# Loading the next block's x in quarters, and one more block with seven products

## The chip, the cores and the metric

The kernel runs on one core of one Trainium2 chip. The metric is device time in microseconds (us), from the start of the program to its end. The kernel before takes 1078.87 us, the median of 3 runs that lie between 1078.11 and 1079.22.

In what follows PE is the matrix engine, DVE, ACT and POOL are the vector, scalar and general engines, and SP is the engine whose only work here is to issue loads from memory. Each engine works through its own instructions in program order and waits on semaphores that the others count up.

## The reference

For 128 samples, x has 64 channels by 512 positions. Each sample picks one of 200 matrices, 64 by 64, and is mixed over its channels with it. A two-layer network follows over the 512 positions, whose weights are first rounded to three values (-1, 0, +1, times one factor alpha per matrix). The result is quantized to 4 bits with one scale for the whole tensor, and x is added:

```
w = weights[conditions];  z = einsum('bct,bcd->bdt', x, w)
h = gelu(einsum('bsd,hd->bsh', z, ternarize(W1)) + b1)      # 512 -> 2048
y = einsum('bsd,hd->bsh', h, ternarize(W2)) + b2            # 2048 -> 512
scale = max(|y|) / 7 + 1e-8
out = x + clip(round(y / scale), -7, 7) * scale
```

The scale needs every y before any output can be written.

## The kernel before, in words

**Tiling.** Two samples make a pair (128 rows), four pairs make a block of 512 token columns, and there are NB = 16 blocks, 0 to 15. The hidden width of 2048 is cut into NH = 16 chunks of 128. The ternary weights stay in on-chip memory in 8 bits and are widened by POOL, chunk by chunk, just before PE uses them (`widen1`, `widen2`, `widen7`). Every activation is held as a high and a low part, so each product is done twice, once with each.

**Memory.** The pool `big` (line 92) has 20 buffers of 8 KB per partition, and `half` (line 94) has 10 of half that size. Each finished block leaves its y in one big buffer until the end. So the later the block, the fewer big buffers are free.

**Layer 1 in two forms.** `eight` (line 881) does one hidden chunk at a time in the plain way: 8 matmuls of 512 columns for layer 1 and 8 for layer 2 (LAG = 2 chunks behind). `pair` with `seven` (lines 938 and 815) does two hidden chunks at a time and takes layer 1 as a product of 2 by 2 matrices of quarters, with seven products in place of eight (Winograd's form of Strassen's method): 28 matmuls of 256 columns for layer 1, and the same 16 of 512 columns for layer 2. I call one such call a step; a block has 8 of them, k = 0 to 7. `SEVEN` (line 88) says which blocks are done so: 2 to 11 here. A seven-block needs three big buffers for its inputs (`parts7`: `xb` and two `xt`, the sums `t` in high and low part) and one half buffer (`xl`); an eight-block needs two big ones (`parts`). The combined weights of the seven products, `w1s`, are one more big buffer.

**The next block's input.** While block n is computed, block n + 1 is prepared. SP loads its x, four pairs at once, into one big buffer (`load_x`, two transfers of 512 KB). POOL gathers the four pairs' matrices (`fetch`) and places them (`place`). Then, one pair in each of four steps, PE mixes the pair's x with its matrix into a PSUM tile `pc` (`mix`: four matmuls of the program, which the profile shows as eight records), and ACT and DVE take the parts from it: `condition` (line 232) for an eight-block, `condition7` (line 783) for a seven-block. `condition7` first copies one quarter of `pc`, `b12`, and forms four sums of quarters, `t`. They lie in a half buffer named `mixed` that all pairs share (lines 923 to 925). It then returns a last piece of work, which splits `t` into its high and low part. Inside a seven-block that piece is kept in `parting` and done one step later.

**Order.** Nothing is scheduled by a tool: the class `InOrder` (line 49) keeps every engine's instructions in the order of the source. In `pair`, the function `behind(i)` (line 953) puts the side work at six places of a step. For the change these matter: at i = 0 of step 0 the load of the next x and its buffers; at i = 2 the kept split of the pair before; at i = 4 of steps 3 to 6 the conditioning of pairs 0 to 3. In `eight` the load stands at chunk 0 and the conditioning at chunks 8 to 11, there with the split done at once.

**The end.** After block 15 the scale is found, and then all 16 blocks are quantized, added to x, which is loaded once more, and written.

Of the kernel before, what the change touches and what calls it, by code (L numbers as in the profile page):

```python
# [28 lines left out]
F32 = mybir.dt.float32  # L29
# [10 lines left out]
P = 128  # L40
# [17 lines left out]
def tile_cond_ternary_ffn(  # L58
# [26 lines left out]
    GH = NH // NG  # L85
    WCH = GH * T
    LAG = 2
    SEVEN = range(2, 12)
    HALF = BLK // 2

    const = ctx.enter_context(tc.tile_pool(name="const", bufs=1))
# [13 lines left out]
    def load_x(n):  # L105

        xt = big.tile([P, PAIRS, T], F32, tag="big", name=f"xt_{n}")
        for h in range(2):
            js = pair_of_pairs(h)
            sp.dma_start(out=xt[:, js, :], in_=x_blk[n][:, js, :])  # L110
        return [xt[:, pair_of_pairs(h), :] for h in range(2)]
# [7 lines left out]
    def split_x(n):  # L119

        return [half_x(n, h) for h in range(2)]
# [94 lines left out]
    def split(src, hi, lo, engine=dve):  # L216

        act.copy(hi, src)
        engine.tensor_tensor(lo, src, hi, ALU.subtract)

    def mix(xt, j, pc):

        for c in range(NT):
            pe.matmul(
                out=pc[:, c, :],
                lhsT=xt[j // 2][:, j % 2, c * P : (c + 1) * P],
                rhs=diag[:, j, :],
                start=True,
                stop=True,
            )  # L230

    def condition(n, j, xt, two):
        pc = ps_c.tile([P, NT, P], F32, tag="pc", name=f"pc_{n}_{j}")
        mix(xt, j, pc)
        split(pc, *(t[:, :, j * P : (j + 1) * P] for t in two))


# [115 lines left out]

    def mix0(j):
        pc = ps_y.tile([P, NT, P], F32, tag=f"py{j}", name=f"pc_0_{j}")
        mix(x_next, j, pc)
        pcs.append(pc)

    def hi0(j):
# [357 lines left out]
    for hc in range(NH - LAG):  # L717
        if hc + 2 < NH - LAG:
            widen2(0, hc + 2)
        layer2(0, hc)  # L720
        g, i = divmod(hc, GH)
        if g + 1 < NG and i in (1, 2):
            turn2(g + 1, i - 1, signs2[g + 1][:, 1, :])(act)
        if g + 2 < NG:
            if i == 0:
                made[g + 2] = signed2(g + 2)
            if i in (0, 2):
                next(made[g + 2])
        if hc in (1, 3, 5, 7):
            condition(1, hc // 2, x_next, two_next)  # L730
        if 8 <= hc < 8 + NG:
            sum2(hc - 8)
    cond[1] = two_next
# [46 lines left out]
            half.tile([P, 2, 2, HALF], F32R, tag="half", name=f"xl_{n}"),  # L780
        )

    def condition7(n, j, xt, two):

        xb, xts, xl = two
        cols = slice(j * C, (j + 1) * C)
        pc = ps_c.tile([P, NT, P], F32, tag="pc", name=f"pc_{n}_{j}")
        mix(xt, j, pc)
        t, b12 = extra["t"], extra["b12"]
        act.copy(b12, pc[:, :2, C:])  # L790
        act.copy(xb[:, 0, :, cols], pc[:, :, :C])
        act.copy(xl[:, 0, :, cols], pc[:, 2:, C:])
        dve.tensor_tensor(t[:, 0], b12, pc[:, :2, :C], ALU.subtract)
        dve.tensor_tensor(t[:, 2], pc[:, 2:, C:], b12, ALU.subtract)
        dve.tensor_tensor(t[:, 1], pc[:, 2:, C:], t[:, 0], ALU.subtract)
        dve.tensor_tensor(t[:, 3], pc[:, 2:, :C], t[:, 1], ALU.subtract)
        dve.tensor_tensor(xb[:, 1, :, cols], pc[:, :, :C], xb[:, 0, :, cols], ALU.subtract)
        dve.tensor_tensor(xl[:, 1, :, cols], pc[:, 2:, C:], xl[:, 0, :, cols], ALU.subtract)
        t8 = t.rearrange("p a c d -> p (a c) d")
        hi, lo = (x.rearrange("p a c d -> p (a c) d")[:, :, cols] for x in xts)  # L800
        return lambda: split(t8, hi, lo)

    def product(out, w, b, first):
        for c in range(2):
# [76 lines left out]
    def eight(s):  # L881

        n, hc = steps[s]
        if s + 1 < len(steps):
            ahead = steps[s + 1]
            if ahead[0] not in SEVEN:
                widen1(*ahead)
                lend(0, *ahead)
            else:
                for g in (2, 3, 0):  # L890
                    widen7(0, g)
        widen2(*steps[s + 1 - LAG])
        lend(1, *steps[s + 1 - LAG])
        if n + 1 < NB:
            if hc == 0:
                x_next.append(load_x(n + 1) if n + 1 < NB - 1 else split_x(n + 1))
                two_next.append(parts7(n + 1) if n + 1 in SEVEN else parts(n + 1))
            if 2 <= hc < 2 + PAIRS:
                fetched.append(fetch(n + 1, hc - 2))
            if 7 <= hc < 7 + PAIRS:  # L900
                place(hc - 7, fetched[hc - 7 - PAIRS])
        if n == NB - 1 and hc == 0:
            again.append(load_x(0))
        if n == NB - 1 and hc in (1, 2):
            again.append(split_x(hc))
        ph = ps_h.tile([P, BLK], F32, tag="ph", name=f"ph_{n}_{hc}")
        layer1(n, hc, ph)
        two = half.tile([P, 2, BLK], F32R, tag="half", name=f"h_{n}_{hc}")
        bend(n, hc, ph, [two[:, k, :] for k in range(2)], hf[hc % 2])
        if s + 1 < len(steps) and steps[s + 1][0] in SEVEN and n not in SEVEN:  # L910
            widen7(0, 1)
        if n + 1 < NB and 8 <= hc < 8 + PAIRS:
            if n + 1 in SEVEN:
                condition7(n + 1, hc - 8, x_next[-1], two_next[-1])()
            else:
                condition(n + 1, hc - 8, x_next[-1], two_next[-1])
            cond[n + 1] = two_next[-1]
        if hc == LAG:
            for j in range(PAIRS):
                largest(n - 1, j)  # L920
        if n + 1 == SEVEN[0]:
            if hc == 2:
                mixed = half.tile([P, 2, BLK], F32, tag="half", name="mixed")
                extra["t"] = mixed[:, 0].rearrange("p (a c d) -> p a c d", a=4, c=2)
                extra["b12"] = mixed[:, 1, : 2 * C].rearrange("p (c d) -> p c d", c=2)
                extra["making"] = combine()
            if hc in (3, 4, 5, 6):
                next(extra["making"])
        if s == len(steps) - 1:
            return  # L930
        if s == NH + 1:
            alpha_2()
        layer2(*steps[s - LAG])
        if steps[s - LAG][1] == NH - 1:
            for j in range(PAIRS):
                result(n - 1, j)

    def pair(n, k, finish):

        s = n * NH + 2 * k  # L940
        ahead = (k + 1) % (NH // 2)
        leaves = ahead == 0 and n + 1 not in SEVEN
        before = steps[s - 2], steps[s - 1]

        def second(i):
            layer2(*before[i // PAIRS], [i % PAIRS])

        def results(js):
            if before[1][1] == NH - 1:
                for j in js:  # L950
                    result(n - 1, j)

        def behind(i):
            if i == 0:
                finish()
                widen2(*before[1])
                if k == 0:
                    x_next.append(load_x(n + 1))
                    two_next.append(parts7(n + 1) if n + 1 in SEVEN else parts(n + 1))
            if i == 1:  # L960
                low(*before[1])
                if leaves:
                    widen1(n + 1, 0)
                else:
                    widen7(ahead, 1)
                    widen7(ahead, 0)
                if k < PAIRS:
                    fetched.append(fetch(n + 1, k))
                if 2 <= k < 2 + PAIRS:
                    place(k - 2, fetched[PAIRS * (n - 1) + k - 2])  # L970
            if i == 2:
                if parting:
                    parting.pop()()
                widen2(*steps[s])
                if not leaves:
                    widen7(ahead, 2)
            if i == 3:
                results(range(2))
            if i == 4:
                if not leaves:  # L980
                    widen7(ahead, 3)
                if 3 <= k < 3 + PAIRS:
                    if n + 1 in SEVEN:
                        parting.append(condition7(n + 1, k - 3, x_next[-1], two_next[-1]))
                    else:
                        condition(n + 1, k - 3, x_next[-1], two_next[-1])
                    cond[n + 1] = two_next[-1]
                if k in (1, 2):
                    for j in (2 * k - 2, 2 * k - 1):
                        largest(n - 1, j)  # L990
            if i == 5:
                results(range(2, PAIRS))

        return seven(n, k, behind, second)

    s = NH
# [110 lines left out]
```

## Time and profile before

| What | Value |
|---|---|
| profiled execution, its own time | 1079.13 us |
| its span, first to last instruction | 1077.4 us |
| median of 3 runs | 1078.87 us |
| PE busy | 999.9 us, 93% of the span |
| DVE, ACT, POOL busy | 594.8, 598.6, 613.8 us (55 to 57%) |
| PE clock granted, mean over the span | 0.969 |
| last matmuls of block 15 end | about 1010 us |
| quantizing, second load of x, output | about 1013 to 1077 us |

The profile is one execution. Its time is 1.7 us longer than its span, which is what lies around the first and last instruction. Busy time is a union over an engine's instructions. A matmul's record covers its start to its modelled end, and ends overlap the next start, so the pace of PE is read from starts. "Idle before" is time in which the engine did nothing, with the engine that ended it. Transfers are shown with the time from issue to landing. All lines of the kernel go through one helper (line 54), so instructions are told apart by the names of their tiles: `xy` and `z` are the accumulators of the seven products, `ph` that of an eight-block's layer 1, `py` those of layer 2, `pc` that of the mix, `mixed` the buffer with the sums.

### The profile page before, as it was taken

To read this page: it belongs to the slowest core of one execution; us is meant where nothing else is said; L and a number is where in the kernel's file an instruction comes from. 1 tells how busy PE (TensorE), PEld (TensorE's weight loads), DVE (VectorE), ACT (ScalarE), POOL (GpSimd) and SP (SyncE) were. 2 spreads that over 40 slices of the span, in tenths; PEclk is the share of its full clock that TensorE was granted. 3 is DMA by queue.
4 is the path that set the end of the run, shared out by engine and by line. 5 is a ranking of instruction groups with operands and counts; after the bars stand their busy time and mean duration, and the time that the engine had idled before them with its cause. 6 is when DMAs were issued, how large, how long until landed. Compare 5 with 4: busy or idle time off the path is not lost.

```text
span 1077.4 us, 16522 instructions
## 1 busy us (share of the span) xinstructions
PE 999.9 (93%) x5778; PEld 867.2 (80%) x5780; DVE 594.8 (55%) x1035; ACT 598.6 (56%) x1010; POOL 613.8 (57%) x996
## 2 busy tenths in 40 slices
PE   7999999999999999999999999999999999999400
PEld 4778788999999999999999999999888888888300
DVE  6985845565665566665656556564423223231692
ACT  6865345666666565656656665665443443433481
POOL 4574836666676757666666667575534435333242
PEclk9999999999999999999999999999999999999855
DMA  9202010010100010010101000100200010041799
GB/s 326 87 17 101 5 40 5 2 43 3 42 4 2 5 41 5 1 44 2 43 4 41 5 1 6 40 5 2 82 2 2 4 40 6 1 145 32 283 413 376
DMA packets 28802, 62.22 MB, mean 58 GB/s; under 512 B 2848, under 2 KB 2992, under 8 KB 28720
## 3 DMA queue, kind: packets, MB, share of 16 engines
q1 hardware_dynamic: 22064, 42.28, 11.4%
q0 software_dynamic: 6656, 18.88, 4.5%
q8 instruction: 47, 0.77, 0.3%
q14 instruction: 35, 0.29, 0.1%
HBM read 44.38 MB, written 16.78 MB: 57 GB/s over the span
## 4 chain that ended last, share of the span: by engine, by line
PE 89%; DMA 5%; DVE 4%; ACT 1%; issue 1%; POOL 0%; SPq 0%; POOLq 0%; DVEq 0%; ACTq 0%
PE py L54 43%; PE ph L54 15%; PE xy L54 14%; PE z L54 11%; PE pc L54 5%; DMA xt<-in_x 3%; DVE top L54 1%; DMA out<-y 1%; DMA nat<-in_L_ffn_W 1%; DVE tern L54 1%; PE pt L54 1%; DVE y L54 0%; DVE h L54 0%; ACT ring L54 0%; ACT diag L54 0%
## 5 line engine op out<-in xcount | busy, mean ns | idle before, releaser
L54 PE MATMUL py<-wf,h 128*128 128x512 f32 x2048 | 530.6, 395 | 1.4 <-ACT h L54 0.7
L54 PEld LDWEIGHTS py<-wf,h 128*128 128x128 f32 x2048 | 366.2, 189 | 67.3 <-DVE y L54 2.3
L54 DVE TENSOR_TENSOR h<-ring,h 128x512 fp32r<-128x512 f32 x249 | 191.8, 771 | 227.9 <-ACT h L54 227.9
L54 POOL CAST wf<-w2t 128x512 fp32r<-128x512 fp8e4 x256 | 185.3, 726 | 176.2 <-PE py L54 160.6
L54 POOL CAST wf<-w1t 128x512 fp32r<-128x512 fp8e4 (+1 forms) x255 | 172.5, 682 | 78.0 <-PE ph L54 57.4
L54 PE MATMUL ph<-x,wf 128*128 128x512 f32 (+1 forms) x776 | 192.4, 391 | 1.8 <-POOL wf L54 0.7
L54 ACT ACTIVATE ring<-ring,b1t,alpha_w 128x512 f32<-128x512 f32 x160 | 131.2, 820 | 88.8 <-DVE ring L54 88.8
L54 POOL CAST wf<-w1s 128x256 fp32r<-128x256 fp8e4 (+1 forms) x240 | 122.2, 514 | 99.4 <-PE xy L54 72.7
L54 ACT ACTIVATE ring<-ph,b1t,alpha_w 128x512 f32<-128x512 f32 x96 | 74.9, 780 | 176.3 <-PE ph L54 174.7
L54 PEld LDWEIGHTS ph<-x,wf 128*128 128x128 f32 x776 | 144.5, 188 | 33.3 <-POOL wf L54 1.3
L54 ACT CAST h<-ring 128x512 fp32r<-128x512 f32 x256 | 158.9, 621 | 8.3
L54 DVE TENSOR_TENSOR ring<-xy,ring 128x256 f32<-128x256 f32 (+1 forms) x160 | 88.3, 552 | 58.9 <-PE xy L54 58.9
L54 PEld LDWEIGHTS xy<-xt,wf 128*128 128x128 f32 x640 | 97.8, 189 | 12.8
L54 PE MATMUL xy<-xb,wf 128*128 128x256 f32 x640 | 101.9, 281 | 0.0
L54 PE MATMUL xy<-xt,wf 128*128 128x256 f32 x640 | 101.7, 282 | 0.0
L54 PEld LDWEIGHTS xy<-xb,wf 128*128 128x128 f32 x640 | 92.7, 190 | 7.1
L54 ACT COPY ring<-xy 128x256 f32<-128x256 f32 x160 | 59.1, 370 | 61.6 <-PE xy L54 61.6
L54 PE MATMUL z<-xt,wf 128*128 128x256 f32 x640 | 89.4, 282 | 0.0
L54 ACT COPY ring<-z 128x512 f32<-128x512 f32 x80 | 47.0, 588 | 66.9 <-DVE h L54 63.7
L54 PEld LDWEIGHTS z<-xt,wf 128*128 128x128 f32 x640 | 82.0, 190 | 0.0
L54 POOL DMA_INDIRECT wg<-in_L_cond_weights,rows x64 | 72.3, 1130 | 13.8 <-issue 5.4
L54 DVE TENSOR_TENSOR xt<-mixed,xt 128x512 fp32r<-128x512 f32 x40 | 30.7, 767 | 81.8 <-ACT xt L54 81.8
(111 smaller groups left out, 825.6 us busy)
## 6 DMA issues: line engine op xcount, KB each, us to landing
xt<-in_x SPq DMA_DIRECT2D x60, 512.0 KB, 5.2
out<-y POOLq DMA_DIRECT2D x30, 512.0 KB, 12.8
nat<-in_L_ffn_W SPq DMA_DIRECT2D x6, 1024.0 KB, 14.7
nat<-in_L_ffn_W SPq DMA_DIRECT2D x3, 512.0 KB, 11.4
wg<-in_L_cond_weights,rows POOLq DMA_INDIRECT x64, 2.6
w1t<-in_x SPq DMA_DIRECT2D x4, 256.0 KB, 2.6
w2t<-in_x SPq DMA_DIRECT2D x4, 256.0 KB, 2.7
out<-xt POOLq DMA_DIRECT2D x2, 512.0 KB, 8.5
```

What stands on the lines that cost most here:

```text
L54: return lambda *args, **kw: self._tc.keep_in_program_order(make(*args, **kw))
```

## The change

Three things are done together.

1. The load of the next block's x is cut into four transfers of one pair (256 KB) each. They go into a half buffer, `x_quarters`, that takes the place of `mixed`. Pair j lands in half j % 2 of it. The big buffer that held x is no longer taken for blocks 2 to 13.
2. After a pair is mixed, its x is dead, and `condition7` writes its sums `t` over it. The copy `b12` lies in the last quarter of `t`, which is written last. So pair j + 2 can be loaded only when pair j's sums have been split.
3. `SEVEN` goes from blocks 2 to 11 to blocks 2 to 12. Block 12's x is prepared by `condition7` and its layer 1 is done by `seven`; the buffers left over by point 1 hold it.

In `pair` the first two quarters are issued at step 1, i = 2, and the third and fourth at steps 4 and 5, i = 2, right after the kept split of pairs 0 and 1. In block 1, which prepares the first seven-block, they are issued at chunk 0 and after the conditioning at chunks 8 and 9.

```diff
-    SEVEN = range(2, 12)
+    SEVEN = range(2, 13)
...
+    def pair_of(xt, j):
+        return xt[j // 2][:, j % 2, :]
...
-                lhsT=xt[j // 2][:, j % 2, c * P : (c + 1) * P],
+                lhsT=xp[:, c * P : (c + 1) * P],
...
-        t, b12 = extra["t"], extra["b12"]
+        t = xp.rearrange("p (a c d) -> p a c d", a=4, c=2)
+        b12 = t[:, 3]
...
+    def quarter_x(n, j):
+
+        sp.dma_start(out=extra["x"][:, j % 2, :], in_=x_blk[n][:, j, :])
...
             if hc == 0:
-                x_next.append(load_x(n + 1) if n + 1 < NB - 1 else split_x(n + 1))
+                if n + 1 == SEVEN[0]:
+                    extra["x"] = half.tile([P, 2, T], F32, tag="half", name="x_quarters")
+                    for j in range(2):
+                        quarter_x(n + 1, j)
+                else:
+                    x_next.append(load_x(n + 1) if n + 1 < NB - 1 else split_x(n + 1))
...
             if n + 1 in SEVEN:
-                condition7(n + 1, hc - 8, x_next[-1], two_next[-1])()
+                condition7(n + 1, j, extra["x"][:, j % 2, :], two_next[-1])()
+                if j + 2 < PAIRS:
+                    quarter_x(n + 1, j + 2)
...
-                mixed = half.tile([P, 2, BLK], F32, tag="half", name="mixed")
-                extra["t"] = mixed[:, 0].rearrange("p (a c d) -> p a c d", a=4, c=2)
-                extra["b12"] = mixed[:, 1, : 2 * C].rearrange("p (c d) -> p c d", c=2)
...
-                    x_next.append(load_x(n + 1))
...
                 if parting:
                     parting.pop()()
+                if k == 1:
+                    quarter_x(n + 1, 0)
+                    quarter_x(n + 1, 1)
+                if k in (4, 5):
+                    quarter_x(n + 1, k - 2)
...
+                    xp = extra["x"][:, (k - 3) % 2, :]
```

More of the change, by code (lines that the diff above doesn't have):

```diff
@@ L219, in split, with mix @@
         engine.tensor_tensor(lo, src, hi, ALU.subtract)
-    def mix(xt, j, pc):
+    def pair_of(xt, j):
+        return xt[j // 2][:, j % 2, :]
+    def mix(xp, j, pc):
         for c in range(NT):
@@ L230, in mix, with condition @@
             )
-    def condition(n, j, xt, two):
+    def condition(n, j, xp, two):
         pc = ps_c.tile([P, NT, P], F32, tag="pc", name=f"pc_{n}_{j}")
-        mix(xt, j, pc)
+        mix(xp, j, pc)
         split(pc, *(t[:, :, j * P : (j + 1) * P] for t in two))
@@ L355, in mix0 @@
         pc = ps_y.tile([P, NT, P], F32, tag=f"py{j}", name=f"pc_0_{j}")
-        mix(x_next, j, pc)
+        mix(pair_of(x_next, j), j, pc)
         pcs.append(pc)
@@ L729, in tile_cond_ternary_ffn @@
         if hc in (1, 3, 5, 7):
-            condition(1, hc // 2, x_next, two_next)
+            condition(1, hc // 2, pair_of(x_next, hc // 2), two_next)
         if 8 <= hc < 8 + NG:
@@ L781, in parts7, with condition7 @@
         )
-    def condition7(n, j, xt, two):
+    def condition7(n, j, xp, two):
         xb, xts, xl = two
@@ L787, in condition7 @@
         pc = ps_c.tile([P, NT, P], F32, tag="pc", name=f"pc_{n}_{j}")
-        mix(xt, j, pc)
-        t, b12 = extra["t"], extra["b12"]
+        mix(xp, j, pc)
+        t = xp.rearrange("p (a c d) -> p a c d", a=4, c=2)
+        b12 = t[:, 3]
         act.copy(b12, pc[:, :2, C:])
@@ L912, in eight @@
         if n + 1 < NB and 8 <= hc < 8 + PAIRS:
+            j = hc - 8
             if n + 1 in SEVEN:
-                condition7(n + 1, hc - 8, x_next[-1], two_next[-1])()
+                condition7(n + 1, j, extra["x"][:, j % 2, :], two_next[-1])()
+                if j + 2 < PAIRS:
+                    quarter_x(n + 1, j + 2)
             else:
-                condition(n + 1, hc - 8, x_next[-1], two_next[-1])
+                condition(n + 1, j, pair_of(x_next[-1], j), two_next[-1])
             cond[n + 1] = two_next[-1]
@@ L982, in behind @@
                 if 3 <= k < 3 + PAIRS:
+                    xp = extra["x"][:, (k - 3) % 2, :]
                     if n + 1 in SEVEN:
-                        parting.append(condition7(n + 1, k - 3, x_next[-1], two_next[-1]))
+                        parting.append(condition7(n + 1, k - 3, xp, two_next[-1]))
                     else:
-                        condition(n + 1, k - 3, x_next[-1], two_next[-1])
+                        condition(n + 1, k - 3, xp, two_next[-1])
                     cond[n + 1] = two_next[-1]
```

## The prediction

> **What bounds the kernel now.** I read the page first: the busy shares, the slices and the chain that ended last.
>
> ```profile
> PE 999.9 (93%) x5778; PEld 867.2 (80%) x5780; DVE 594.8 (55%) x1035; ACT 598.6 (56%) x1010; POOL 613.8 (57%) x996
> PE   7999999999999999999999999999999999999400
> PE 89%; DMA 5%; DVE 4%; ACT 1%; issue 1%; POOL 0%; SPq 0%; POOLq 0%; DVEq 0%; ACTq 0%
> ```
>
> PE fills every slice from the second to the fourth last, and 89% of the chain is PE. So the blocks are worth what PE's instructions in them take. Next I asked for the busy times in two windows, block 11 (the last with seven products) and block 12 (the first with eight again). Columns: window, length, then busy time and count of PE, PEld, DVE, ACT, POOL, the granted clock, the share of DMA and GB/s.
>
> ```profile
> 701.40:761.10 59.70, 59.70 (x386) 54.28 (x384) 31.14 (x53) 35.59 (x62) 37.20 (x66) 1.00 0.06 21
> 761.10:823.00 61.90, 61.90 (x290) 51.54 (x289) 20.12 (x31) 25.79 (x38) 26.85 (x44) 1.00 0.07 20
> ```
>
> PE is never idle in either, the clock is full, and the others are at most 62% busy. The edges come from the timeline of PE, where a block starts with its first layer 1 group:
>
> ```profile
> 701.37 0.63 PE L54 MATMUL xy<-xb,wf 128*128 128x256 f32 x4
> 761.10 1.99 PE L54 MATMUL ph<-x,wf 128*128 128x512 f32 x8
> 822.96 1.75 PE L54 MATMUL ph<-x,wf 128*128 128x512 f32 x7
> ```
>
> Block 11 takes 761.10 - 701.37 = 59.73 us, block 12 takes 822.96 - 761.10 = 61.86. The other blocks agree: block 2 starts at 163.63, so ten seven-blocks take 597.47 us, 59.75 each; block 14 starts at 884.83, so block 13 takes 61.87. **One seven-block in place of an eight-block is worth 2.12 us.** This is the number that the forecast stands on.
>
> **What the Trainium skill says.** "TensorE: Matmul & The Clock Gate", section "Back-to-back issue gap", gives an isolated gap of N / 2.4 + 2.5 ns: 109 ns for 256 columns, 216 for 512. From that, 28 x 109 against 16 x 216 would save 0.40 us a step, an estimate of 3.2 us a block. The trace does not agree at 256 columns: four matmuls of 256 start 0.46 to 0.47 us before the next group (701.37 to 701.83), 117 ns each, and eight of 512 start 1.82 us before it (761.10 to 762.92), 227 ns. The measured block length decides. On transfers, "DMA: Bandwidth & Descriptors", section "Anatomy of one DMA", fits 2.0 us plus bytes / 436e3 (for transfers issued by the general engine), an estimate of 2.6 us for 256 KB. The trace has eight loads from SP of just this size and row shape, one pair of x each, landing in 2.5 to 2.8 us. The same section says that a semaphore is waited for on the issuing sequencer and not in the DMA engines. So a load that waits for a split holds SP's queue, and nothing else.
>
> **The change, part by part.**
>
> *Block 12 with seven.* Two eight-chunks take 768.36 - 761.10 = 7.26 us (starts of `ph`), a step of seven without a mix takes 708.39 - 701.37 = 7.02. Eight times 0.24 is 1.92. An eight-block also loses 0.18 us at its third chunk (3.81 us between starts, not 3.63), where layer 2 waits for DVE to empty `py`; a seven-block doesn't. Sum 2.10, against 2.12 from the edges. I take 2.12. Mixes are equal on both sides (4 x 0.9 us). POOL, DVE and ACT get more to do in block 12, up to block 11's 37.2, 31.1 and 35.6 us of 59.7: PE covers it. The sums for block 12 are added to block 11's side work, where seven-blocks that prepare a seven-block already stand at the same 59.75. The return to eight, with its change of weights, moves from 11/12 to 12/13 and costs what it did.
>
> *Loads.* Four issues of 0.33 us replace two of 0.44 in twelve blocks, on an SP that does nothing else there. POOL's queue isn't touched by them. The first two quarters wait for the last block's splits, half a block ago, and have two steps (14 us) to land. What matters is pairs 2 and 3. Lines from the timeline of block 8, and from the summaries of the 256 KB loads into `w1t` and `w2t`:
>
> ```profile
> 564.34 0.74 DVE L54 TENSOR_TENSOR xt<-mixed,xt 128x512 fp32r<-128x512 f32 x1 [2.23 <-ACT xt L54]
> 573.48 0.72 PE L54 MATMUL pc<-diag,xt 128*128 128x128 f32 x5
> ...
> DMA to landing us min/median/max: 2.5/2.6/2.7
> DMA to landing us min/median/max: 2.7/2.7/2.8
> ```
>
> The first is the split of pair 1, which frees the half for pair 3, at 565.08. The second is pair 3's mix. Room 8.4 us, need 2.8: 5.6 us to spare, so 0 us. In block 1 there are no kept splits and the steps are shorter, so there it is tightest:
>
> ```profile
> 136.84 0.69 DVE L54 TENSOR_TENSOR xt<-mixed,xt 128x512 fp32r<-128x512 f32 x1 [0.16 <-ACT xt L54]
> 141.31 0.69 DVE L54 TENSOR_TENSOR xt<-mixed,xt 128x512 fp32r<-128x512 f32 x1 [0.16 <-ACT xt L54]
> 141.65 1.08 PEld L54 LDWEIGHTS pc<-diag,xt 128*128 128x128 f32 x8
> ```
>
> Pair 0 is split at 137.53, and pair 2's x is wanted as weights at 141.65: room 4.12 us, need about 2.8, 1.3 to spare. Pair 3: freed at 142.00, wanted at 146.18, the same room. Cover gone means PE stands still for the lateness, once, since pair 3 moves with it. DMA carries next to nothing there (the share in the blocks is 0.05 to 0.07). I take 0.
>
> *Added waits.* The mixes of pairs 1 and 3 now wait for a load of their own: 24 waits on PE's queue, with all of PE behind them. Such a satisfied wait costs between 0 and the distance that the trace shows between mixes with and without one. Before, pairs 0 and 2 have it and 1 and 3 don't, and the four mixes of block 11 start at 728.95, 736.87, 744.79 and 752.71, 7.92 apart each. So 0; I keep 0.1 us x 24 = 2.4 as the far end. DVE and ACT also get a wait for the load before they write the sums over it; that load has landed before the mix could run. ACT's copy of `b12` must now wait for all four mix matmuls, which its next copy of `pc` did already.
>
> *Buffers.* A big buffer per block is given back. Blocks 11 and 12 fill all 20 again (3 weights, 3 + 3 or 3 + 2 inputs, 11 or 12 y), but each y goes where an input of the block before lay, read by PE before that block ended. No y waits for a load any more. The waits of the last stage's loads are on the same work as before. That stage takes its start from PE's end, so it is shifted whole. I take 0; a different choice of buffers could move it by some tenths either way.
>
> *Sum.* Profiled execution: 1079.13 - 2.12 = 1077.0, span 1077.4 - 2.1 = 1075.3. From the median, which is 0.26 lower: 1078.87 - 2.12 = **1076.75 us**.
>
> **Rivals.**
> - *The gain is eaten in part, within 0.2%.* The quarters in block 1 come 2 us later than I think (a landing of over 4.1 us; median for 512 KB is 5.2), or the added waits cost 0.05 us or more each. For: the room of 1.3 us is the smallest here. Against: all eight 256 KB loads landed by 2.8, and the even spacing of mixes. Time 1077.5 to 1079.
> - *Slower: PE waits for the quarters in every block.* Pairs 2 and 3 can't be loaded ahead, and a load that takes over 8.4 us from its release stalls PE in each of the ten blocks 2 to 11 as well as in block 1. At 9 us: 0.6 x 10 there, 4.9 in block 1, less 2.1, so some 1088 us. It decides from about 8.4 us, where block 1 alone gives 4.3 - 2.1 = 2.2 slower. For: in the last stage loads take up to 26 us. Against: there the DMAs are full, here they are empty.
> - *Faster than arithmetic.* If the seven-block gave what the skill's gaps say, 3.2 us: 1075.7. Ten measured blocks speak against it.
>
> **How the numbers follow.** This kernel's runs spread over 1.1 us, so 0.2%, 2.16 us, is about what a measurement can tell from no change. My forecast of 2.12 lies on that bound. The likeliest case has 0.78, with its own range 1076.1 to 1077.4; it splits nearly evenly between faster and same. The first rival has 0.10 (same), the second 0.09 (slower), the third 0.03 (faster). With an allowance for small shifts of buffers towards the gain this makes faster 0.45, same 0.45, slower 0.10. The range 1075.9 to 1078.3 takes in the likeliest case, the third rival in part and half of the first.
>
> **What would show it.** Right: block 12 is 59.75 us between PE's starts, 2.1 less; blocks 2 to 11 stay at 59.75; PE has no idle time before `pc` that a load of x ended; in block 1 the mixes still start 9.06 us apart from pair 0 to pair 2; the stage after PE's end keeps its 67 us. Wrong: PE or its weight loads idle on `x_quarters`, loads of over 4 us in the blocks, or a last stage that is longer than before.

## The result

The changed kernel takes 1076.76 us, the median of 20 runs between 1076.32 and 1077.65. The kernel before, in 20 runs beside it, takes 1078.28 us (1077.93 to 1079.23). The ratio is 0.9985 with a 95% interval of 0.9978 to 0.9992. So it is shorter by 1.5 us, and the interval stays clear of no change; but that is 0.15%, less than the 0.2% from which the prediction would have called it faster. The median hits the forecast of 1076.75 almost exactly, but the gain is smaller than the forecast 2.12 us: the kernel before itself measured 0.6 us lower over 20 runs than over the 3 runs known at the time.

The page of the changed kernel, the same three lines as before:

```profile
PE 997.6 (93%) x5876; PEld 869.5 (81%) x5876; DVE 612.9 (57%) x1083; ACT 611.2 (57%) x1046; POOL 628.4 (58%) x1020
...
PE   7999999999999999999999999999999999999400
...
PE 88%; DMA 4%; DVE 4%; ACT 2%; issue 1%; POOL 0%; SPq 0%; POOLq 0%; DVEq 0%; ACTq 0%
```

PE loses 2.3 us of busy time, while DVE, ACT and POOL gain 13 to 18 us each. That is the trade of one seven-block for one eight-block, and PE is still the engine that fills the blocks.

Busy times in windows, with the columns as before: blocks 11 and 12, now both with seven products, and block 13.

```profile
700.50:760.20 59.70, 59.70 (x385) 54.34 (x384) 36.50 (x77) 36.91 (x73) 40.06 (x69) 1.00 0.08 21
760.20:820.00 59.80, 59.80 (x386) 54.35 (x384) 31.59 (x53) 35.65 (x62) 37.41 (x66) 1.00 0.12 34
820.00:881.90 61.90, 61.90 (x290) 51.54 (x289) 20.11 (x31) 25.79 (x38) 26.85 (x44) 1.00 0.07 20
```

The starts of these blocks in the timeline of PE:

```profile
700.50 0.63 PE L54 MATMUL xy<-xb,wf 128*128 128x256 f32 x4
...
760.24 0.63 PE L54 MATMUL xy<-xb,wf 128*128 128x256 f32 x4
...
820.00 1.99 PE L54 MATMUL ph<-x,wf 128*128 128x512 f32 x8
...
881.88 1.98 PE L54 MATMUL ph<-x,wf 128*128 128x512 f32 x8
```

Block 11 takes 59.74 us, block 12 takes 59.76 (61.86 before), block 13 takes 61.88. Block 12 is shorter by 2.10 us, and no other block paid for it.

The quarters. First block 1, with the timeline rows that answer to those of before (pairs 0 and 1 split, pair 2 loaded as weights); then block 8, where the first row is pair 1's split and the last is pair 3's mix; then the landing times of the loads of quarters. The trace has a landing for 30 of these 48.

```profile
136.01 0.69 DVE L54 TENSOR_TENSOR xt<-x_quarters,xt 128x512 fp32r<-128x512 f32 x1 [0.16 <-ACT xt L54]
...
136.78 13.87 SPq L54 DMA_DIRECT2D x_quarters<-in_x  x4
...
140.83 1.08 PEld L54 LDWEIGHTS pc<-diag,x_quarters 128*128 128x128 f32 x8
...
563.51 0.74 DVE L54 TENSOR_TENSOR xt<-x_quarters,xt 128x512 fp32r<-128x512 f32 x1 [2.22 <-ACT xt L54]
...
572.65 1.06 PE L54 MATMUL pc<-diag,x_quarters 128*128 128x128 f32 x8
...
DMA to landing us min/median/max: 2.5/2.7/3.1
```

In block 1 pair 0's split ends at 136.70, the load of pair 2 is issued at 136.78, and it is wanted at 140.83. Landing took 2.5 us there, so it was in time by 1.5 us. In block 8 the split of pair 1 ends at 564.25, so the room is 8.4 us again to the mix, 8.3 to its first weight load at 572.53. PE shows no idle time in the blocks: between 120 and 990 us no matmul has a gap of over 0.03 us before it. The gain is where it was forecast; what is open is why the medians show less of it.

### The profile page after: what moved, and what is told of

The parts are those of the page before. It is cut to its first block, busy times and chain, and to the rows that moved or that the text cites. A ratio compares the mean times of both kernels' runs of the same rounds, so it can differ in the third digit from the quotient of the medians.

```text
span 1074.9 us, 16962 instructions
## 1 busy us (share of the span) xinstructions
PE 997.6 (93%) x5876; PEld 869.5 (81%) x5876; DVE 612.9 (57%) x1083; ACT 611.2 (57%) x1046; POOL 628.4 (58%) x1020
## 4 chain that ended last, share of the span: by engine, by line
PE 88%; DMA 4%; DVE 4%; ACT 2%; issue 1%; POOL 0%; SPq 0%; POOLq 0%; DVEq 0%; ACTq 0%
PE py L54 43%; PE xy L54 16%; PE z L54 12%; PE ph L54 12%; PE pc L54 5%; DMA xt<-in_x 2%; DVE top L54 1%; DMA out<-y 1%; DMA nat<-in_L_ffn_W 1%; DVE y L54 1%; ACT diag L54 1%; DVE tern L54 1%; PE pt L54 0%; ACT junk L54 0%; DVE h L54 0%
## 5 line engine op out<-in xcount | busy, mean ns | idle before, releaser
L54 ACT ACTIVATE ring<-ring,b1t,alpha_w 128x512 f32<-128x512 f32 x176 | 144.4, 820 | 97.6 <-DVE ring L54 97.6
L54 POOL CAST wf<-w1s 128x256 fp32r<-128x256 fp8e4 (+1 forms) x264 | 134.4, 514 | 109.5 <-PE xy L54 80.4
L54 PE MATMUL ph<-x,wf 128*128 128x512 f32 (+1 forms) x648 | 160.0, 390 | 1.4 <-POOL wf L54 0.7
L54 PEld LDWEIGHTS ph<-x,wf 128*128 128x128 f32 x648 | 120.0, 188 | 27.6 <-POOL wf L54 1.3
L54 ACT ACTIVATE ring<-ph,b1t,alpha_w 128x512 f32<-128x512 f32 x80 | 62.4, 780 | 138.8 <-PE ph L54 137.7
L54 PEld LDWEIGHTS xy<-xt,wf 128*128 128x128 f32 x704 | 107.6, 189 | 14.0
L54 PE MATMUL xy<-xb,wf 128*128 128x256 f32 x704 | 112.1, 281 | 0.0
L54 PE MATMUL xy<-xt,wf 128*128 128x256 f32 x704 | 111.8, 282 | 0.0
L54 PEld LDWEIGHTS xy<-xb,wf 128*128 128x128 f32 x704 | 102.0, 190 | 7.8
L54 DVE TENSOR_TENSOR xt<-x_quarters,xt 128x512 fp32r<-128x512 f32 x44 | 33.8, 768 | 90.7 <-ACT xt L54 90.7
```

Of the source, the lines that this page charges most:

```text
L54: return lambda *args, **kw: self._tc.keep_in_program_order(make(*args, **kw))
```

## Experiments

Eleven kernels were run. Eight were timed in several runs, in two groups that each shared runs of the kernel before; in the first group that one took 1077.39 us (50 runs), in the second 1078.19 (49 runs). The first group ran on one chip of the machine and the second on another, so each kernel is compared with the runs of before in its own group. The three kernels with repeated loads ran once each, on the first group's chip.

### The changed kernel again

No edit.

> The changed kernel once more, to see how its gain splits over the span. My theory (one seven-block is worth 2.12 us in the blocks, and nothing else of the change costs or gains): median 2.1 us under the kernel before, blocks 2 to 12 at 59.75 us each, the head up to block 2 and the stage after PE's end scattered by some tenths around before's 163.6 and 67.2 us. Rival (loading in quarters costs about 0.5 us outside the blocks): median 1.5 to 1.6 us under before, with a longer head or last stage in the trace again.

Measured: 1075.48 us (21 runs), ratio 0.9983 (0.9976 to 0.9989), 1.9 us under before. Blocks as in the first trace. The medians' gain now lies between the two theories (2.1 us, and 1.5 to 1.6); the trace is used in the table below. It has landings for 42 loads: one of the two that are issued at 29 us in the head, among the weights' loads, took 7.7 us, and all others 2.5 to 3.1.

### Loading in quarters alone, and the worth of a seven-block

```diff
-    SEVEN = range(2, 13)
+    SEVEN = range(2, 12)      # second kernel: range(2, 11)
```

> Loading in quarters alone, with seven products in blocks 2 to 11 as before. My theory: no difference from the kernel before, within 0.3 us, and block 12 at 61.86 us again. Rival (quarters cost 0.5 us outside the blocks): 0.4 to 0.6 us slower than before. Rival (the quarters stall PE): blocks 2 to 11 longer than 59.75 us.

> Loading in quarters with one seven-block fewer than before, blocks 2 to 10. It sets the worth of one seven-block by time. My theory: 2.1 us slower than the run with quarters alone and 4.2 us slower than the changed kernel. Rival (a seven-block is worth only what the medians showed): 1.5 us slower per block, 3.0 us over the changed kernel.

Measured: 1078.00 us for quarters alone, ratio 1.0006 (0.9998 to 1.0014), and 1080.02 for blocks 2 to 10, ratio 1.0024 (1.0015 to 1.0033). From the changed kernel over the first to the second, the medians rise by 2.52 and 2.02 us, 2.27 a block on average. The medians put a seven-block at about what PE's starts say, and the theory of 1.5 us a block falls. Quarters alone came out 0.6 us over before, with 1.0 just inside the interval: more than the 0.3 us that my theory allowed, and what the rival of a cost had forecast. Its block 12 is an eight-block of the old length again:

```profile
759.28 1.08 PE L54 MATMUL ph<-x,wf 128*128 128x512 f32 x4
...
821.14 0.62 PE L54 MATMUL ph<-x,wf 128*128 128x512 f32 x2
```

That is 61.86 us. So the 0.6 us, if it is there, is not in the blocks. The other half of the pair, seven products in block 12 with x in a big buffer, was not tried: by a count of the buffers, block 11 would then need 21 of 20 big ones.

### The first two quarters later

```diff
             if hc == 0:
-                if n + 1 == SEVEN[0]:
-                    extra["x"] = half.tile(...)
-                    for j in range(2):
-                        quarter_x(n + 1, j)
...
+            if hc == 4:
+                extra["x"] = half.tile(...)
+                for j in range(2):
+                    quarter_x(n + 1, j)
```

> The changed kernel, but the buffer is taken and the first two quarters for block 2 are issued at chunk 4 of block 1, not at chunk 0, whose place in SP's queue lets them go at 29.6 us among the weights' loads. If these two early loads cost the head something (a rival for where 0.5 us went), this is 0.3 to 0.6 us faster than the changed kernel and its block 2 starts earlier. My theory: no difference within 0.3 us; they land long before chunk 8 in both.

Measured: 1075.80 us (16 runs), ratio 0.9985 (0.9978 to 0.9993); against the changed kernel's 1075.48 in the same group it is 0.3 us over, not under. The two early loads cost the head nothing that shows in the time.

### How much room the quarters have

Loads of pairs 2 and 3 are repeated. Each repeat overwrites the same half, so it waits on SP for the one before to land.

```diff
-        sp.dma_start(out=extra["x"][:, j % 2, :], in_=x_blk[n][:, j, :])
+        for _ in range(2 if j >= 2 else 1):      # 3 and 4 in the other two kernels
+            sp.dma_start(out=extra["x"][:, j % 2, :], in_=x_blk[n][:, j, :])
```

> Every load of pairs 2 and 3 is done twice, one after the other, so that x lands about 5.4 us after its half is released and not 2.7. My theory (room 4.1 us in block 1, 8.3 us in the blocks with seven): in block 1 PE waits 1.2 to 1.4 us once, before the mix of pair 2, and nowhere else; span 1.3 us over the changed kernel's. Rival (the room isn't what sets it, some other wait covers it): no idle time of PE in front of a mix, span as the changed kernel's.

> Pairs 2 and 3 loaded three times in a row, landing about 8.1 us after the release. My theory: about 4.0 us of waiting in block 1 before pair 2 and up to 0.8 more before pair 3, and in the ten blocks 2 to 11 the loads just fit into the room of 8.3 us, so at most 0.2 us each; span 4.8 to 7 us over the changed kernel's. Rival (the blocks' room is smaller than I read, for instance 5.6 us): 2.5 us of waiting in every block, span 25 us or more over.

> Pairs 2 and 3 loaded four times in a row, landing about 10.8 us after the release. My theory: the room is overrun in every block: 2.4 to 2.8 us of waiting in each of blocks 2 to 11, 10 us in block 1, less in block 12, where a half is released by the mix alone; span 34 to 40 us over the changed kernel's. Rival (only block 1 is tight): about 10 us over.

PE's waits in the three, from the view of who waited for whom (total, times, longest), in the order two, three, four loads:

```profile
PE pc L54 <- DMA x_quarters<-in_x: 0.7, 1, 0.7
```

```profile
PE pc L54 <- DMA x_quarters<-in_x: 4.7, 3, 3.4
```

```profile
PE pc L54 <- DMA x_quarters<-in_x: 30.0, 16, 6.2
```

*Twice*: one wait, in block 1 before pair 2. Its mix started 5.42 us after that of pair 1 and not 4.53, so 0.9 us late, a little under the 1.2 to 1.4 expected: a repeated load is issued 2.55 us after the one before, so two land 5.1 us after the release, not 5.4. The span, 1074.8 us, is 1.1 over the changed kernel's second trace and 0.1 under its first, so it settles nothing at this size. *Three times*: the mixes of pairs 2 and 3 of block 1 were late by 3.6 and 1.2 us, 4.8 together, as expected, and in the ten blocks 2 to 11 there was one wait of 0.24 us; the stretch from block 2 to PE's end was 0.9 us longer than the changed kernel's. The span was 1079.7 us, 6.0 over the changed kernel's second trace and 4.8 over its first. *Four times*: blocks 2 to 11 all stall. They took 62.65 to 63.65 us each and lost 34.9 together, 3.5 a block; block 12, where a half is released by the mix alone, kept its 59.75. Block 1 lost 10.1 us (6.33 and 3.73), as expected. The span was 1118.3, 43.5 to 44.6 over, more than the 34 to 40 expected.

What was missing in that expectation is not the waiting. Of the 30.0 us that PE waited for loads, 6.2 fall into block 1 and 23.8 into the ten blocks: 2.4 a block, as expected. (Every block waited about 2 us before pair 2. Blocks 2, 4, 6, 8 and 10 waited again before pair 3, for 0.4 to 1.2 us: its loads stood on SP behind the fourth load of pair 2.) The rest is for the most part PE's clock. In each of blocks 3, 5, 7, 9 and 11 the granted clock fell to half for 3.41 us, 0.6 to 0.9 us after the wait before pair 2 had ended, and in block 1 for 6.83 us, from within that wait. Block 3, in windows before, in and after that stretch (window, length, PE's busy time and count, granted clock, the share of DMA and GB/s):

```profile
278.40:280.70 2.30, 0.20 (x2) 1.00 0.64 216
281.35:284.65 3.30, 3.30 (x16) 0.50 0.27 79
284.80:290.20 5.40, 5.40 (x35) 1.00 0.30 97
```

Five stretches at half clock cost the blocks up to 8.5 us, an estimate from 5 x 3.41 / 2; with the 23.8 that makes 32.3 of the 34.9. Not every wait brought one: none followed in the other five blocks, nor in the kernel with three loads, which waited 3.4 and 1.0 us in block 1. What decides it, these traces do not show.

The two rooms are what the trace of before gave, 4.1 and 8.3 us. The added waits themselves cost nothing that can be seen as long as the load has landed.

### Scatter or a cost of the quarters

Four more kernels ask where the 0.6 us of quarters alone came from. The second takes the half buffer for the sums two chunks earlier in the kernel before; the third and fourth issue the first two quarters at step 2, in the changed kernel and in quarters alone.

```diff
 # kernel before, in eight()
             if hc == 0:
+                if n + 1 == SEVEN[0]:
+                    mixed = half.tile([P, 2, BLK], F32, tag="half", name="mixed")
...
             if hc == 2:
-                mixed = half.tile([P, 2, BLK], F32, tag="half", name="mixed")
...
 # changed kernel, in pair()
-                if k == 1:
+                if k == 2:
                     quarter_x(n + 1, 0)
```

> The kernel before, unchanged, for the scatter of the measurement and of its head and last stage. Quarters alone showed 0.6 us over before, with the blocks as before. Theory of scatter (each build's head, last stage and the time outside the span move by some tenths): this run is within 0.4 us of the shared runs of before, its last stage between 67.2 and 67.7 us. Theory of a cost (quarters cost 0.5 us in head or last stage): its last stage is 67.2 us again, 0.3 to 0.5 shorter than in the four runs with quarters.

> The kernel before, with the half buffer for the sums taken at chunk 0 of block 1 and not at chunk 2, where the changed kernel takes its own. No instruction is added; only which half buffers the h tiles of block 1 get, and so a few waits, differ. Theory of scatter: 0 to 0.5 us off before in either direction. Theory of a cost of the quarters: no difference to before, under 0.2 us.

> The changed kernel with its first two quarters issued at step 2, not step 1; they still land 6 us before they are wanted. My theory: as the changed kernel within 0.4 us, blocks at 59.75 us. Under a cost of the quarters nothing changes either; the run gives a second build of the changed kernel, and its difference to the first is the scatter.

> Quarters alone (seven in blocks 2 to 11), with the first two quarters issued at step 2: a second build of quarters alone. Theory of scatter: between 0.3 us under and 0.7 us over before, not the same 0.6 over. Theory of a cost: 0.5 to 0.7 us over before once more. In both, 2.1 us over the run before it for the one seven-block that is missing, give or take the scatter.

Measured, with the ratio to the shared runs of before (1078.19 us): before again 1078.12, 1.0000 (0.9992 to 1.0008); sums buffer early 1078.20, 1.0000 (0.9992 to 1.0009); changed with step 2 1076.74, 0.9985 (0.9978 to 0.9991); quarters alone with step 2 1078.39, 1.0001 (0.9993 to 1.0010). The second build of quarters alone is 0.2 us over before, so a cost of 0.5 us did not come back; but it ran on the other chip, and the first build was not run again, so whether that one's 0.6 us was scatter or its own stays open. The second build lies 1.65 us over the changed kernel with step 2, where 2.1 was expected, give or take the scatter. Nor did the sums' buffer show any scatter in the median, which fits both theories. The kernel before, run again, has a last stage of 67.91 us in its trace, longer than either theory had it (67.2 to 67.7), so the longer last stages of the kernels with quarters need no cost of the quarters.

Each trace cut in three, at the start of block 2 (first `xy`) and the end of the last layer 2 group; the fourth number is their sum, the span. One execution each, in us:

| Kernel | to block 2 | block 2 to PE's end | last stage | span |
|---|---|---|---|---|
| before | 163.63 | 846.50 | 67.24 | 1077.37 |
| before again | 162.76 | 846.36 | 67.91 | 1077.03 |
| sums buffer early | 162.80 | 846.36 | 67.23 | 1076.39 |
| quarters alone | 161.78 | 846.52 | 67.71 | 1076.01 |
| quarters alone, step 2 | 162.95 | 846.35 | 67.30 | 1076.61 |
| quarters, blocks 2 to 10 | 161.82 | 848.61 | 67.59 | 1078.01 |
| changed | 162.81 | 844.37 | 67.68 | 1074.86 |
| changed again | 161.82 | 844.34 | 67.54 | 1073.71 |
| changed, step 2 | 162.24 | 844.32 | 68.05 | 1074.61 |
| changed, first quarters late | 161.44 | 844.75 | 67.45 | 1073.64 |

The middle column moves with the number of seven-blocks, and but for one kernel by at most 0.2 us otherwise: its means are 846.42 over the five kernels with ten seven-blocks and 844.34 over the three first ones with eleven, 2.08 us less; with nine it is 848.61, 2.19 more. (The fourth with eleven lies 0.4 higher; step 1 of its block 12 alone took 7.27 us and not 7.02, which its trace puts down to no wait on x.) The outer columns move by up to 2.2 and 0.8 us from kernel to kernel and execution to execution; the kernel before alone gave 67.24 and 67.91 in the last stage. A part of it goes with the chip: the four traces from the first group's have 161.4 to 161.8 us to block 2, the four from the second's 162.2 to 163.0. In the second group those with quarters (162.95 and 162.24) lie on both sides of those without (162.76 and 162.80); the first group has no trace of the kernel before to compare with, and for the first comparison's two traces no chip is on record.

A second place where time went is outside the span. Per kernel, the mean of all its timed runs less the mean of their spans is 1.76 and 1.77 us for before in the two groups, 1.76 to 1.77 for quarters alone, its second build and the sums buffer early, but 1.97, 1.95 and 2.00 for the changed kernel in the first comparison, again, and with step 2. That is 0.2 us of the gain. The kernel with the first quarters late has 1.83 and the one with blocks 2 to 10 has 2.12, so it goes neither with the quarters nor with the number of seven-blocks. What it is, the profile does not show.

The means of the spans fell by 1.98 us in the first group (1075.63 to 1073.65) and by 1.82 in the second (1076.49 to 1074.67). So of 2.08 us in the blocks, 1.8 to 2.0 reach the span, and 1.6 to 1.8 reach the mean time (1077.39 to 1075.60 and 1078.26 to 1076.67). The 0.1 to 0.3 us between blocks and span is within what the outer columns scatter and stays open.

## Why the prediction was right

- **The worth of a seven-block** held. Block 12 went from 61.86 to 59.76 us, and the stretch from block 2 to PE's end lost 2.08 us in the means of the table, against 2.12 forecast. Taking the measured block length was the choice that mattered. The isolated gaps in "TensorE: Matmul & The Clock Gate" of the Trainium skill, section "Back-to-back issue gap", gave an estimate of 3.2 us. Even the 117 and 227 ns that the prediction read at the head of two blocks would give only an estimate of 2.8: over the seven-blocks of the changed kernel's trace the median distance between starts is 120 ns at 256 columns and 231 at layer 2's 512, where the eight-blocks have 227.
- **POOL, DVE and ACT under PE** held: in block 12 they went up to 37.4, 31.6 and 35.7 us of 59.8, and PE has no idle time there.
- **The loads at 0 us** held. In the blocks they landed in 2.5 to 3.1 us where the trace has a landing, and rooms of 4.1 and 8.3 us are what the repeated loads found. The rival with a stall in every block has its threshold where it was put: three loads, some 7.7 us, barely touch the blocks, and four, some 10.3 us, stall each of the ten. It misjudged the size beyond the threshold: it counted one late pair a block, where in every second block a second one came late behind SP's queue, and in the others PE lost time at half clock after the wait.
- **The added waits at 0** held: the far end of 2.4 us would stand in the middle column, where quarters alone (846.52 and 846.35) are equal to before (846.50 and 846.36).
- **The last stage "shifted whole"** held only within its scatter. A longer last stage was named as a sign of being wrong, and in the first trace it is 0.4 us longer (67.68 against 67.24); the kernel before, run again, has 67.91, so this sign could not tell at that size. The term that was mis-sized is the step from the blocks' gain to the time: the sum took it as 1 to 1, and 0.2 us went outside the span, with 0.1 to 0.3 more unresolved in the head and the last stage. So the gain measured 1.5 to 1.9 us in three comparisons and not 2.1.
- **The base.** That the median came out at 1076.76 although the gain was smaller is luck of the base: three runs of before gave 1078.87, twenty gave 1078.28.
- **The chances**, even between faster and same, reflected a forecast that lay on the bound. The measured 0.15% is on the side of the same, with an interval that reaches over the bound (0.22%) and stays clear of no change (0.08%).

## What to carry to other kernels

Where PE fills every slice, price an exchange of one block form for another by the distance between PE's starts of such blocks in the trace; here that was right to 0.04 us, while the price from isolated matmul gaps was 1.1 us too high. In these runs a buffer that is reused sooner cost nothing as long as the room between its release and its next use was longer than the load, and that room can be read from two lines of the timeline before a line is changed; look for the one place where the pipeline is shorter, here the block that prepares the first of its kind. Beyond the room the loss can be more than the waiting: with four loads ten blocks waited 23.8 us and lost 34.9. When a forecast is of the size of 0.2%, split the traces at fixed places: the part that the change touches showed the effect in every single execution, while the whole times had to be taken over a dozen or more runs. Compare heads and ends of traces from one chip only.

## What the runs showed that was not expected

The time outside the span is steady for one build (1.97 and 1.95 us for the changed kernel in two comparisons, 1.76 and 1.77 for before) and differs between builds that differ in a few instructions (1.76 to 2.12), so a span's gain need not be the whole time's. A wait of PE of about 2 us was followed in five of ten blocks by 3.41 us at half the granted clock, so a stall can go on costing after it has ended. A load of 256 KB that waits for the one before it follows at 2.55 us, so the wait on SP and the issue add nothing that can be seen to the landing of 2.5 to 2.6 us.
